# Masked attention over kept tokens on one core: seven half-size products for the outputs of batches 0 to 5, and another order of the work around the last batch

## The chip, the core and the metric

The kernel runs on one core of one Trainium2 chip. A core has engines with queues of their own: TensorE (PE in the profile; PEld is its loading of weights), VectorE (DVE), ScalarE (ACT), GpSimd (POOL) and SyncE (SP), which here only issues DMAs. Each engine takes its instructions in program order, and semaphores between them carry the dependences. TensorE's results go to PSUM, eight banks of 128 partitions by 512 floats; ScalarE and VectorE read them from there. All data are 32-bit floats. The metric is the device time of one execution in microseconds, as the median of several runs.

## The reference

The input x has 8 batches of 512 features by 1024 tokens, with a mask of zeros and ones over the tokens, about half of them one. Queries, keys and values are one and the same projection, for 8 heads of 64 features:

```python
xt = jnp.transpose(x, (0, 2, 1))
q = xt @ Wq.T
qh = q.reshape(B, T, NH, dk).transpose(0, 2, 1, 3)
scores = scale * jnp.einsum('bhqd,bhkd->bhqk', qh, qh)
cmask = mask[:, None, None, :]
rmask = mask[:, None, :, None]
logits = (scores * cmask + (1.0 - cmask) * NEG) * rmask
attn = jax.nn.softmax(logits, axis=-1)
ctx = jnp.einsum('bhqk,bhkd->bhqd', attn, qh)
ctx = ctx.transpose(0, 2, 1, 3).reshape(B, T, D)
out = ctx @ Wo.T          # returned transposed, and added to x
```

A token whose mask is one attends to the tokens whose mask is one. For a token whose mask is zero all logits are zero, so its row is the mean over all tokens, the same for all of them.

## The kernel before

**Kept tokens.** Only the kept tokens of a batch and one more, the mean, are computed: `NK` = 544 places (`SHORT`). A second build of the same function for 576 places (`LONG`) and a kernel for all tokens stand behind checks on the device and are not executed with these data. The last 32 of the 544 places are `END`; `sizes` is 128, 128, 128, 128, 32, and index `LAST` = 4 means the 32.

**The way of a batch.** x is turned (VectorE), stored to DRAM (`xd`), and the kept rows are gathered back (`gather`, GpSimd's queue). `collect` turns them on TensorE into `xc`, features by tokens. The work then goes by pairs of heads, four pairs a batch, 32 in all, numbered (batch, pair) from (0, 0) to (7, 3). Per pair: `project` (128 features of q, in two halves of 272 tokens), `turn_values`, `lengths_of` and `bias_of` (an upper bound on the scores for the exponential), `scores` with the exponentials on ScalarE (tile `e`, sums beside it), `begin_attend`, `go_on_attend` and `end_attend` (weights times values, to `cT`, 128 features by 544 tokens). `inverses` and `invert` take the inverse sums by way of DRAM to a tile `rb`, and `contexts` multiplies `cT` by it on VectorE. The last two pairs use `spread` instead, which brings the inverses to all partitions with small matmuls.

**Outputs.** `output(b, i)` takes 128 tokens (or the last 32): for each of the four `cT` of the batch a matmul of tokens by 512 output columns, accumulated in one PSUM bank, a ScalarE copy to a tile `oc`, and a store to `od` in DRAM by GpSimd's queue. The 32 tokens use four column tiles of the array, 128 output columns each. Every matmul of 32-bit floats appears as two MATMUL instructions in the profile. Later `load_rows` (SyncE) fetches x in tokens by features into tiles `g`, `fetch` (GpSimd, adding while it gathers) adds the rows of `od`, `finish_blocks` turns the sums on VectorE, and SyncE stores 2 MB to the output. For a batch b this happens in batch b + 2 (`FETCH`, `FINISH`, `ROWS`), for batch 6 in batch 7 (`FETCH_LAST`, `FINISH_LAST`, `ROWS_LAST`). The outputs of batch 7 are begun in the last pair over three of the four `cT` (`begin_output`, tile `pa`) and finished with the fourth (`end_output`); then eight gathers (`fetch_last`), TensorE transposes, the sum with x and eight stores (`finish_tokens`) end the kernel.

**The order.** It is written out by hand. A pair has five slots, k = 0 to 4; slot k begins with the scores of one block of 128 keys (the narrow block `LAST` first, then 0 to 3). `slots_of(p)` lists what else stands in each slot, and the loop in `late` puts around it, in this order: `add_ends` (k = 1), `contexts` and `invert` (k = 0), fetches, gathers, in slot 3 of pairs 1 and 3 four sums over x on ScalarE (`add_features`, line 493), then the slot's list, then loads, searches, `load_rows` and `finish_blocks`. Before each fetch and gather `keep_step` copies one element of `e` on GpSimd, so that the transfer does not start before that slot. The outputs of batch b - 1 stand in batch b: 0, 1 and the narrow one in pair 1, output 2 in pair 2, output 3 in pair 3, always slot 3.

**PSUM.** Scores use four banks (tag `s`). Tags `t` and `a` have two banks each; `bank(name)` takes one of `t` in turn, `a` serves mainly the attention's sums. In the first and the last pairs `t` and `a` are used alternately. A tile in SBUF with `bufs=n` is likewise one of n buffers in turn: `xt` (2), `oc` (5), `xin` (5), `g` (8).

## Time and profile before

| | us |
|---|---|
| median of 3 runs | 651.81 |
| lowest, highest | 649.6, 653.38 |
| the profiled execution | 656.09 |
| its span, first to last instruction | 654.4 |
| TensorE busy in it | 614.3 |
| ScalarE, VectorE, GpSimd busy | 378.3, 359.8, 211.1 |

A row of the timeline gives the start in us from the span's start, the time it took, the engine, the line of the kernel, the operation, what it writes and reads, the shape and the count; in brackets at its end stands how long the engine was idle before it and what ended that wait. Neighbouring rows of one kind are merged, and the time of a merged TensorE row reaches to the modelled end of its last matmul, so the next start is the better measure. A row of a group (no start in front) ends with busy time and mean duration in ns, then the idle time before such instructions. A row of stretches gives the busy time of each engine (count of instructions in brackets) between two times, then the granted clock of TensorE as a share, the share of DMA time and GB/s.

### The profile page before, as it was taken

The page shows a single profiled execution, that of the slowest core. Times are in us where ns is not written, and L with a number is a line of the kernel's source. Part 1 is how long each engine was busy: PE and PEld are TensorE (multiplying, and loading weights), DVE is VectorE, ACT ScalarE, POOL GpSimd, SP SyncE. Part 2 cuts the span into 40 slices and gives each one's busy share as a digit, 9 for nine tenths or more (in the row PEclk, how much of TensorE's full clock was granted, in tenths as well). Part 3 has the DMA queues.
Part 4 walks back from the last instruction along what each step waited for, and adds up shares of the span by engine and source line. Part 5 has one row for each costly group of instructions (what it writes and reads, how often), then busy time and mean ns, then how long its engine had stood idle before and what let it go on. Part 6 is the DMA issues. An engine that isn't in the chain of part 4 may idle for free. (4 is left out here: it accounts for less than half of the span.)

```text
span 654.4 us, 15913 instructions
## 1 busy us (share of the span) xinstructions
PE 614.3 (94%) x6078; PEld 380.5 (58%) x6078; DVE 359.8 (55%) x1034; ACT 378.3 (58%) x1004; POOL 211.1 (32%) x313
## 2 busy tenths in 40 slices
PE   4789799999999999999999999999999999998964
PEld 3756466656665666566665666566665666554323
DVE  6449556335465566746465558566575425444543
ACT  4266558754766577754776577664775556554400
POOL 5620400140067004830176004720275006305422
PEclk7799899999999999999999999999999999999985
DMA  7666612454588757977598756975795635566677
GB/s 237 187 199 166 233 57 67 141 168 133 147 178 214 244 172 186 180 246 230 172 182 257 228 173 155 199 244 187 196 179 164 198 102 94 111 162 188 112 220 219
DMA packets 94543, 116.62 MB, mean 178 GB/s; under 512 B 11911, under 2 KB 61639, under 8 KB 94462
## 3 DMA queue, kind: packets, MB, share of 16 engines
q1 hardware_dynamic: 74030, 75.20, 38.6%
q0 software_dynamic: 16208, 38.25, 25.2%
q10 hardware_dynamic: 4224, 2.10, 1.1%
q8 instruction: 49, 0.80, 0.5%
q14 instruction: 32, 0.26, 0.1%
HBM read 72.81 MB, written 42.70 MB: 177 GB/s over the span
## 5 line engine op out<-in xcount | busy, mean ns | idle before, releaser
L692 ACT ACTIVATE e<-s,bias 128x544 f32<-128x544 f32 x256 | 180.5, 710 | 75.6 <-PE s L684 58.9
L684 PE MATMUL s<-qT 64*64 64x272 f32 x2048 | 154.8, 398 | 6.5 <-ACT e L692 4.9
L748 PE MATMUL av<-e,v 64*64 64x272 f32 x1920 | 132.4, 392 | 0.0
L598 PE MATMUL pq<-xc,wqT 128*128 128x272 f32 x512 | 131.4, 401 | 0.0
L598 PEld LDWEIGHTS pq<-xc,wqT 128*128 128x128 f32 x512 | 93.3, 190 | 36.8 <-issue 21.0
L684 PEld LDWEIGHTS s<-qT 64*64 64x64 f32 x2048 | 77.2, 133 | 55.8 <-ACT e L692 13.4
L883 PE MATMUL po<-woT,cT 128*128 128x512 f32 (+1 forms) x448 | 108.9, 439 | 0.0
L894 POOL DMA_DIRECT2D od<-oc x56 | 30.2, 544 | 238.5 <-ACT oc L892 237.7
L977 POOL DMA_INDIRECT g<-od,block_origin x56 | 90.1, 1610 | 30.9 <-DVE ends L721 8.1
L748 PEld LDWEIGHTS av<-e,v 64*64 64x64 f32 x1920 | 76.6, 134 | 38.1 <-issue 2.1
L664 DVE TENSOR_REDUCE m<-pq 128x1 f32<-128x128 f32 x28 | 8.2, 292 | 132.0 <-ACT qT L610 107.5
L883 PEld LDWEIGHTS po<-woT,cT 128*128 128x128 f32 (+1 forms) x448 | 46.5, 149 | 54.6 <-issue 53.2
L608 ACT COPY qT<-pq 128x272 f32<-128x272 f32 x64 | 24.6, 385 | 69.7 <-PE pq L655 29.0
L947 DVE STREAM_TRANSPOSE xr<-g 128x512 f32<-128x512 f32 x56 | 57.9, 1099 | 7.6 <-DMA g<-od,block_origin 7.5
L645 DVE TENSOR_REDUCE len<-sq 128x10 f32<-128x640 f32 x32 | 25.8, 805 | 60.4 <-ACT sq L643 60.3
L974 POOL COPY step<-e 1x1 f32<-1x1 f32 x75 | 23.7, 316 | 90.7 <-ACT e L692 90.5
L692 ACT ACTIVATION_READ_ACCUMULATOR e<-s,bias 128x1 f32 x256 | 50.5, 197 | 0.0
L544 POOL DMA_INDIRECT xin<-xd,source x40 | 38.7, 968 | 16.6 <-issue 5.6
L892 ACT COPY oc<-po 128x512 f32<-128x512 f32 (+1 forms) x35 | 18.0, 515 | 44.0 <-PE po L883 43.5
L474 DVE STREAM_TRANSPOSE xt<-x 128x1024 f32<-128x1024 f32 x28 | 34.7, 1241 | 1.5 <-DMA xd<-xt 0.9
L532 DVE TENSOR_SCALAR_CACHE_REDUCE junk<-rank,key 128x1024 f32<-128x1024 f32 (+4 forms) x35 | 34.9, 998 | 0.0
L721 DVE CUSTOM_DVE_ANT_0 junk<-el,part 128x272 f32<-128x272 f32 x64 | 27.3, 427 | 6.6 <-ACT el L709 4.4
(175 smaller groups left out, 674.0 us busy)
## 6 DMA issues: line engine op xcount, KB each, us to landing
xd<-xt SPq DMA_DIRECT2D x120, 128.0 KB
x<-in_x_dram SPq DMA_DIRECT2D x56, 256.0 KB
g<-xd SPq DMA_DIRECT2D x56, 256.0 KB
out_dram<-xr SPq DMA_DIRECT2D x28, 512.0 KB
rb<-row SPq DMA_DIRECT2D x60, 160.0 KB
od<-oc POOLq DMA_DIRECT2D x28, 256.0 KB
rank<-ranks SPq DMA_DIRECT2D x6, 512.0 KB
x<-in_x_dram POOLq DMA_DIRECT2D x8, 256.0 KB
```

The source lines that it names most:

```text
L474: nc.vector.transpose(xt.rearrange("p k (d f) -> p k d f", d=ND), xs[b][r][:, :, at : at + n].rearrange("p d (k t) -> p k d t", t=Q),)
L532: nc.vector.tensor_scalar(junk[:, :n], rank[:, i * P :], key[:, col], 0.0, ALU.is_le, ALU.add, accum_out=found[:, col])
L544: nc.gpsimd.indirect_dma_start(out=xin[:n, :], out_offset=None, in_=xds[b], in_offset=bass.IndirectOffsetOnAxis(ap=searches[b][2][:n, i : ...
L598: nc.tensor.matmul(pq[:, :KH], wqT[:, d, pr * P : (pr + 1) * P], xcs[b][:, d, cols], start=(d == 0), stop=(d == ND - 1),)
L684: nc.tensor.matmul(ss[h][r * DK : (r + 1) * DK, hf, :KH], qT[heads[h], c * P + r * DK : c * P + (r + 1) * DK], qT[heads[h], queries[hf]], ...
L692: nc.scalar.activation(e[:, :, h, :], ss[h][:, :, :KH], AF.Exp, bias=bias, scale=SCALE, accum_out=sums[pair[1] % 2][:, h, c : c + 1],)
L721: nc.vector.tensor_tensor_reduce(junk[:, :KH], e[:, 0, h, :], parts[b], 1.0, 0.0, ALU.mult, ALU.add, ends[pr % 2][:, h : h + 1])
L748: nc.tensor.matmul(avs[pair][hf][head, :KH], v[keys, c, head], e[keys, hf, h, :], start=(c == 0 and not crossed), stop=(c == LAST - 1 and ...
L883: nc.tensor.matmul(po[k * n : (k + 1) * n, :w], cTs[b, pr][:, i * P : i * P + n], woT[:, pr, k * w : (k + 1) * w], start=(pr == 0), stop=( ...
L894: nc.gpsimd.dma_start(ods[b][places[i], k * w : (k + 1) * w], oc[k * n : (k + 1) * n, :w])
L947: nc.vector.transpose(xr.rearrange("p (d a) (t i) -> p a d t i", a=A, i=NT)[..., i], gs[b, i].rearrange("p (a d f) -> p a d f", a=A, f=Q),)
L977: nc.gpsimd.indirect_dma_start(out=gs[b, i], out_offset=None, in_=ods[b], in_offset=bass.IndirectOffsetOnAxis(ap=block_origin[:, b, i : i ...
```

## The change

For the build with 544 places, the outputs of batches 0 to 5 (made in batches 1 to 6) are computed for the 512 full places as one product of two 512 by 512 matrices by seven products of quarter matrices (256 tokens x 256 features x 256 columns) and sums before and after. `combine_weights` forms four sums of quarters of the output weights on GpSimd, once, in pair (1, 0). `combine_tokens` forms four sums of quarters of the tokens on VectorE, in slots 1 and 2 of pair 1, into two `xt` tiles. `product(b, i)` computes one product in one bank, as eight MATMUL instructions, and adds it into four tiles c11, c12, c21, c22 (tag `oc`): product 1 is copied by ScalarE, all other sums are VectorE's, reading PSUM; each finished quarter is stored by GpSimd's queue, 256 rows of 256 columns. Products 1, 6, 7, 5 stand in slot 3 of pair 1, then the narrow output, then the projection, which there takes a bank of `a`; products 2 and 3 in pair 2; product 4 in pair 3.

Around the last batch: all outputs of batch 6 are made in pair (7, 1): output 0 in slot 2, outputs 1 and 2 in slot 3, output 3 and the narrow one in slot 4, where before output 2 stood in slot 4 of (7, 1), output 3 in slot 1 and the narrow one in slot 3 of (7, 2). Loads, fetches and transposes of batch 6 move earlier with it. In the last pair the spread and the contexts of the pair before stand in slot 0, not 1, and the five partial products in slots 1, 2, 3, 4, 4, not 1, 1, 2, 3, 4. The partial and the final product of the last 32 tokens use four column tiles of 128 columns, with the columns read in another order, and their store becomes four DMAs on SyncE's and ScalarE's queues in turn.

```diff
@@ -319,6 +319,7 @@
     G = NB // P
     A = P // Q
     NQ = 4
+    in_halves = n == SHORT
     NC = -(-LONG // P)
     LAST = NC - 1
     LP = LAST * P
@@ -893,44 +894,156 @@
         for k in range(parts):
             nc.gpsimd.dma_start(ods[b][places[i], k * w : (k + 1) * w], oc[k * n : (k + 1) * n, :w])
 
+    HALF = D // 2
+    both = {}
+    if n == SHORT:
+        for i in range(1, 5):
+            both["t", i] = keep.tile([P, 2, HALF], F32, name=f"t_{i}")
+
+    def combine_weights():
+
+        left = [woT[:, 0:2, 0:HALF], woT[:, 2:4, 0:HALF]]
+        right = [woT[:, 0:2, HALF:D], woT[:, 2:4, HALF:D]]
+        t1, t2, t3, t4 = (both["t", i] for i in range(1, 5))
+        nc.gpsimd.tensor_tensor(t1, right[0], left[0], ALU.subtract)
+        nc.gpsimd.tensor_tensor(t2, right[1], t1, ALU.subtract)
+        nc.gpsimd.tensor_tensor(t3, right[1], right[0], ALU.subtract)
+        nc.gpsimd.tensor_tensor(t4, t2, left[1], ALU.subtract)
+
+    def combine_tokens(b, i):
+
+        if i in (1, 3):
+            t = sb.tile([P, T // NQ // Q, P], F32, tag="xt", name=f"st_{b}_{i}", bufs=2)
+            t = t.rearrange("p k c -> p (k c)").rearrange("p (s j n) -> p s j n", s=2, j=2)
+            both["s", i], both["s", i + 1] = t[:, 0], t[:, 1]
+        for j in range(2):
+            early, late_ = cTs[b, j], cTs[b, 2 + j]
+            to = both["s", i][:, j, :]
+            upper, lower = slice(0, 2 * P), slice(2 * P, 4 * P)
+            if i == 1:
+                nc.vector.tensor_tensor(to, early[:, lower], late_[:, lower], ALU.add)
+            elif i == 2:
+                nc.vector.tensor_tensor(to, both["s", 1][:, j, :], early[:, upper], ALU.subtract)
+            elif i == 3:
+                nc.vector.tensor_tensor(to, early[:, upper], early[:, lower], ALU.subtract)
+            else:
+                nc.vector.tensor_tensor(to, late_[:, upper], both["s", 2][:, j, :], ALU.subtract)
+
+    def product(b, i):
+
+        def tokens(j, m):
+            cols = slice(m * P, (m + 1) * P)
+            if i in (3, 5, 6, 7):
+                return both["s", {3: 4, 5: 1, 6: 2, 7: 3}[i]][:, j, cols]
+            first = 2 * P if i == 4 else 0
+            cols = slice(first + m * P, first + (m + 1) * P)
+            return cTs[b, j if i == 1 else 2 + j][:, cols]
+
+        def features(j):
+            if i == 1:
+                return woT[:, j, 0:HALF]
+            if i == 2:
+                return woT[:, 2 + j, 0:HALF]
+            if i == 3:
+                return woT[:, 2 + j, HALF:D]
+            return both["t", {4: 4, 5: 1, 6: 2, 7: 3}[i]][:, j, :]
+
+        po = bank(f"po_{b}_{i}")
+        for m in range(2):
+            for j in range(2):
+                nc.tensor.matmul(
+                    po[:, m * HALF : (m + 1) * HALF],
+                    tokens(j, m),
+                    features(j),
+                    start=(j == 0),
+                    stop=(j == 1),
+                )
+
+        def new(name):
+            t = both[name] = sb.tile([P, D], F32, tag="oc", name=f"{name}_{b}", bufs=NC)
+            return t
+
+        def store(t, row, col):
+            rows = slice(END + row * 2 * P, END + (row + 1) * 2 * P)
+            nc.gpsimd.dma_start(
+                ods[b][rows, col * HALF : (col + 1) * HALF].rearrange("(m p) c -> p m c", p=P),
+                t.rearrange("p (m c) -> p m c", m=2),
+            )
+
+        add = nc.vector.tensor_tensor
+        if i == 1:
+            ods[b] = dr.tile([NK, D], F32, tag="od", name=f"od_{b}")
+            nc.scalar.copy(new("c11"), po)
+        elif i == 6:
+            add(new("c12"), po, both["c11"], ALU.add)
+        elif i == 7:
+            add(new("c21"), po, both["c12"], ALU.add)
+        elif i == 5:
+            add(new("c22"), po, both["c21"], ALU.add)
+            add(both["c12"], po, both["c12"], ALU.add)
+            store(both["c22"], 1, 1)
+        elif i == 2:
+            add(both["c11"], po, both["c11"], ALU.add)
+            store(both["c11"], 0, 0)
+        elif i == 3:
+            add(both["c12"], po, both["c12"], ALU.add)
+            store(both["c12"], 0, 1)
+        else:
+            add(both["c21"], both["c21"], po, ALU.subtract)
+            store(both["c21"], 1, 0)
+
     partials = {}
 
+    def add_product(b, i, pr, po, start, stop):
+
+        n = sizes[i]
+        parts = P // n
+        w = D // parts
+        tokens = cTs[b, pr][:, i * P : i * P + n]
+        if parts == 1:
+            nc.tensor.matmul(po, tokens, woT[:, pr, :], start=start, stop=stop)
+            return
+        in_order = woT[:, pr, :].rearrange("p (a d f) -> p d a f", a=A, d=ND)
+        for k in range(parts):
+            nc.tensor.matmul(
+                po[k * n : (k + 1) * n, :w],
+                tokens,
+                in_order[:, k * ND // parts : (k + 1) * ND // parts, :, :],
+                start=start,
+                stop=stop,
+            )
+
     def begin_output(b, i):
 
-        n = sizes[i]
         po = bank(f"pa_{b}_{i}")
         for pr in range(ND - 1):
-            nc.tensor.matmul(
-                po[:n, :],
-                cTs[b, pr][:, i * P : i * P + n],
-                woT[:, pr, :],
-                start=(pr == 0),
-                stop=(pr == ND - 2),
-            )
+            add_product(b, i, pr, po, pr == 0, pr == ND - 2)
+        w = D // (P // sizes[i])
         pa = sb.tile([P, D], F32, tag="xin", name=f"pa_{b}_{i}", bufs=NC)
-        nc.scalar.copy(pa[:n, :], po[:n, :])
+        nc.scalar.copy(pa[:, :w], po[:, :w])
         partials[i] = pa
 
     def end_output(b, i):
         n = sizes[i]
+        parts = P // n
+        w = D // parts
         if i == 0:
             ods[b] = dr.tile([NK, D], F32, tag="od", name=f"od_{b}")
         po = bank(f"po_{b}_{i}")
-        nc.tensor.matmul(
-            po[:n, :],
-            cTs[b, ND - 1][:, i * P : i * P + n],
-            woT[:, ND - 1, :],
-            start=True,
-            stop=True,
-        )
+        add_product(b, i, ND - 1, po, True, True)
         oc = sb.tile([P, D], F32, tag="oc", name=f"oc_{b}_{i}", bufs=NC)
-        nc.vector.tensor_tensor(
-            oc[:n, :].rearrange("p (d a f) -> p a d f", d=ND, a=A),
-            po[:n, :].rearrange("p (a d f) -> p a d f", d=ND, a=A),
-            partials[i][:n, :].rearrange("p (a d f) -> p a d f", d=ND, a=A),
-            ALU.add,
-        )
-        nc.sync.dma_start(ods[b][places[i], :], oc[:n, :])
+        if parts == 1:
+            nc.vector.tensor_tensor(
+                oc.rearrange("p (d a f) -> p a d f", d=ND, a=A),
+                po.rearrange("p (a d f) -> p a d f", d=ND, a=A),
+                partials[i].rearrange("p (a d f) -> p a d f", d=ND, a=A),
+                ALU.add,
+            )
+        else:
+            nc.vector.tensor_tensor(oc[:, :w], po[:, :w], partials[i][:, :w], ALU.add)
+        for k in range(parts):
+            queue = nc.scalar if k % 2 else nc.sync
+            queue.dma_start(ods[b][places[i], k * w : (k + 1) * w], oc[k * n : (k + 1) * n, :w])
 
     def in_blocks(t):
         return t.rearrange("(k f) (a n) -> a f k n", f=Q, a=A)
@@ -1035,12 +1148,25 @@
             do(0, go_on_attend, before)
         due = []
         if pr == 1 and b + 1 == B:
-            due = [0, 1]
-        elif pr > 0 and 0 < b < B - 1:
+            due = [1, 2]
+            do(2, output, b - 1, 0)
+        elif pr > 0 and 0 < b < B - 1 and not in_halves:
             due = {1: (0, 1, LAST), 2: (2,), 3: (3,)}[pr]
+        halves = ()
+        if in_halves and 0 < b < B - 1:
+            halves = ((), (1, 6, 7, 5), (2, 3), (4,))[pr]
+            if pr == 1:
+                for k, i in ((1, 1), (1, 2), (2, 3), (2, 4)):
+                    do(k, combine_tokens, b - 1, i)
         if not new:
+            for i in halves:
+                do(3, product, b - 1, i)
+            if halves and pr == 1:
+                do(3, output, b - 1, LAST)
             for i in due:
                 do(3, output, b - 1, i)
+        if in_halves and p == ND:
+            do(0, combine_weights)
         if p == 0:
             do(0, project, behind, 1)
             do(1, values, behind)
@@ -1070,6 +1196,8 @@
             do(3, collect, b + 1, 3, None, "a")
             do(3, collect, b + 1, 4, by_vector)
             do(3, lengths_of, behind)
+            for i in halves:
+                do(3, product, b - 1, i)
             for i in due:
                 do(3, output, b - 1, i)
             do(3, project_with_top, 0)
@@ -1078,22 +1206,21 @@
             do(1, project_with_values)
             do(2, lengths_of, behind)
             do(2, end_attend, before)
-            do(3, project_with_top, 1)
+            do(3, project_with_top, 1, "a" if halves and pr == 1 else "t")
         elif behind:
-            do(1, output, b - 1, LAST - 1)
             do(1, values, behind)
             do(2, lengths_of, behind)
             do(2, end_attend, before)
             do(3, bias_of, behind)
-            do(3, output, b - 1, LAST)
         if p == ND - 1:
             for d in range(ND):
                 do(3 + d // 2, turn_weights, woT, "wo", d, None, "at"[d // 2], True)
         if pr == 1 and b + 1 == B:
-            do(4, output, b - 1, 2)
+            do(4, output, b - 1, LAST - 1)
+            do(4, output, b - 1, LAST)
         if p + 1 == len(pairs):
             for i in range(NC):
-                do((1, 1, 2, 3, 4)[i], begin_output, b, i)
+                do((1, 2, 3, 4, 4)[i], begin_output, b, i)
         return todo
 
     def load_weights(w, nm, queue=None):
@@ -1300,10 +1427,10 @@
             (1, 1): (6, 7),
         }
         FINISH = {(0, 4): (0, 1), (1, 1): (2, 3), (1, 2): (4, 5), (1, 4): (6, 7)}
-        FETCH_LAST = {(2, 4): (0, 1, 2), (3, 0): (3, 4, 5), (3, 1): (6, 7)}
-        FINISH_LAST = {(3, 1): (0, 1, 2), (3, 2): (3, 4, 5), (3, 3): (6, 7)}
+        FETCH_LAST = {(2, 0): (0,), (2, 1): (1, 2), (2, 2): (3, 4), (2, 3): (5, 6), (2, 4): (7,)}
+        FINISH_LAST = {(2, 3): (0,), (2, 4): (1, 2), (3, 1): (3, 4, 5), (3, 2): (6, 7)}
         ROWS = {(2, 2): (0, 1), (2, 3): (2, 3), (3, 0): (4, 5), (3, 2): (6, 7)}
-        ROWS_LAST = {(2, 0): (0, 1, 2), (2, 1): (3, 4, 5), (2, 2): (6, 7)}
+        ROWS_LAST = {(1, 2): (0, 1), (1, 3): (2, 3), (1, 4): (4, 5), (2, 0): (6, 7)}
         for p, pair in enumerate(pairs):
             b, pr = pair
             before = pairs[p - 1] if p else None
@@ -1319,10 +1446,9 @@
                         invert(before)
                     else:
                         inv = inverses(before)
-                if p + 1 == len(pairs):
-                    if k == 1:
-                        spread(before, inv)
-                        contexts(before)
+                if p + 1 == len(pairs) and k == 0:
+                    spread(before, inv)
+                    contexts(before)
                 if b > 1:
                     for i in FETCH.get((pr, k), ()):
                         keep_step(pair, c)
```

4 lines of the change are left out of this document (2 added, 2 removed).

## The prediction

> **What bounds the kernel now.** I read the page first, then the busy time by stretch, then the timelines of TensorE, ScalarE and VectorE for one batch and for the end. The stretches below are one batch (from its first output product to the next batch's), the last pair, and the tail.
>
> ```profile
> span 654.4 us, 15913 instructions
> PE 614.3 (94%) x6078; PEld 380.5 (58%) x6078; DVE 359.8 (55%) x1034; ACT 378.3 (58%) x1004; POOL 211.1 (32%) x313
> ...
> core 0: us, PE busy (x) PEld busy (x) DVE busy (x) ACT busy (x) POOL busy (x), PEclk, DMA share, GB/s
> 200.36:272.67 72.31, 72.06 (x755) 44.72 (x751) 44.62 (x127) 46.79 (x127) 25.81 (x37) 1.00 0.74 203
> ...
> 597.50:631.20 33.70, 30.75 (x180) 12.90 (x180) 18.25 (x37) 10.41 (x26) 13.31 (x15) 1.00 0.71 135
> 631.20:654.40 23.20, 8.96 (x33) 5.80 (x33) 6.49 (x15) 0.00 (x0) 7.64 (x8) 0.54 0.72 219
> ```
>
> A middle batch (here batch 2's products to batch 3's) takes 72.31 us and TensorE is busy for 72.06 of them, at a granted clock of 1.00. So matmul time saved there is time saved, and a wait added to TensorE is time lost, one for one. Only the last pair (33.70 us, 30.75 busy) and the tail have slack. The profiled execution took 656.09 us for its span of 654.4; the median of the runs is 651.81, 0.7% below, and I carry differences over to it.
>
> **Products: what they save.** TensorE in batch 6 (pairs 1 and 3) and in batch 7:
>
> ```profile
> 489.44 8.14 PE L883 MATMUL po<-woT,cT 128*128 128x512 f32 x48
> 497.51 2.10 PE L598 MATMUL pq<-xc,wqT 128*128 128x272 f32 x8
> ...
> 531.27 3.70 PE L883 MATMUL po<-woT,cT 128*128 128x512 f32 x8
> 534.81 2.00 PE L598 MATMUL pq<-xc,wqT 128*128 128x272 f32 x8
> 536.64 0.27 PE L655 MATMUL pq<-ident,top 128*128 128x128 f32 x1
> ...
> 561.69 7.13 PE L883 MATMUL po<-woT,cT 128*128 128x512 f32 x16
> 568.66 2.00 PE L598 MATMUL pq<-xc,wqT 128*128 128x272 f32 x8
> 588.59 1.08 PE L883 MATMUL po<-woT,cT 128*32 128x128 f32 x32
> 589.60 1.15 PE L684 MATMUL s<-qT 64*64 64x272 f32 x16
> ```
>
> From start to next start, sixteen instructions of 512 columns take 6.97 us, eight take 3.54, so one takes 0.43 and about 0.1 goes to the change of tile shape; eight of 272 columns take 1.83 (229 ns each). For 256 columns I take 214 ns, half of 427 and just below the line through the two; the upper bound is 229, if weight loads set the pace. A product is 2 token blocks x 2 feature chunks x 2 instructions = 8, so 1.71 us. Seven make 12.0 against 13.65 for the four outputs (32 x 427): 1.7 us saved per batch, 10.2 over six. By place: pair 1 gives up two outputs for four products (0), pair 2 one for two (0), pair 3 one for one (-1.71). At 229 ns the saving is 0.85 per batch, 5 in all.
>
> The Trainium skill ("TensorE: Matmul & The Clock Gate", section Back-to-back issue gap) gives a warm gap of N/2.4 + 2.5 ns. If each instruction is two passes, an estimate from that page is 432 and 218 ns, which would save 1.6 us per batch instead of 1.7 and make the sum below 0.6 us later; the trace's 229 ns for 272 columns agrees with the page's 232.
>
> **Products: what they wait for.** They use two banks in turn ("t"); a bank is free once its product is evacuated. A bank used to be wanted every 3.5 us, now every 1.71. ScalarE, then VectorE, during slots 1 to 3 of pair 1 of batch 6; the last VectorE row is the second pair of transposes in batch 2:
>
> ```profile
> 491.00 0.62 ACT L493 ACTIVATE junka<-x 128x512 f32<-128x512 f32 x1
> ...
> 493.79 0.18 ACT L493 ACTIVATION_READ_ACCUMULATOR junka<-x 128x1 f32 x1
> 493.88 0.56 ACT L892 COPY oc<-po 128x512 f32<-128x512 f32 x1
> ```
>
> ```profile
> 487.99 2.05 DVE L947 STREAM_TRANSPOSE xr<-g 128x512 f32<-128x512 f32 x2
> ...
> 490.75 2.04 DVE L947 STREAM_TRANSPOSE xr<-g 128x512 f32<-128x512 f32 x2
> 500.32 0.29 DVE L664 TENSOR_REDUCE m<-pq 128x1 f32<-128x128 f32 x1 [7.53 <-ACT qT L610]
> ...
> 202.65 2.04 DVE L947 STREAM_TRANSPOSE xr<-g 128x512 f32<-128x512 f32 x2
> ```
>
> The four L493 sums stand ahead of the output copies in slot 3. Product 1 ends 1.8 us after 489.44, but its copy to c11 cannot start before 493.88 and ends at +5.0. Products 1 and 6 have filled both banks by +3.5, so product 7 starts at +5.05: a wait of 1.5 us in each of six batches.
>
> Then VectorE, on which eight new sums of 128x256 stand in slots 1 and 2. The nearest prices:
>
> ```profile
> 623.43 0.38 DVE L800 TENSOR_TENSOR cT<-av,rb 128x272 f32<-128x272 f32 x1
> 625.75 0.44 DVE L800 TENSOR_TENSOR cT<-av,rb 128x272 f32<-128x272 f32 x1 [1.95 <-PE av L730]
> L927 DVE TENSOR_TENSOR oc<-po,pa 128x512 f32<-128x512 f32 x4 | 2.8, 691 | 1.1 <-PE po L919 1.1
> L401 POOL TENSOR_SCALAR part<-count,kept 64x272 f32<-64x272 f32 x16 | 15.5, 970 | 5.3 <-DMA xin<-xd,source 4.7
> ```
>
> At 0.40 us (between the two L800 rows; 0.32 if they overlap, 0.46 if each waits for the one before) they add 3.2 us. The transposes of slot 2, which stand before product 6's sum, end at 492.79 - 489.44 = +3.35 now and at +6.5 then; in batch 2, whose products start at 200.36, they end at +4.33 now and +7.5 then. The sum needs 0.7 (L927) and frees the bank of product 5. So product 5 starts at about +8.2 in batch 2, +7.9 in 4 (nearly as late), +7.3 in 6, and at +6.8, right behind product 7, where the transposes come earlier (3, 5) or are absent (1). From there 1.71 for it and 0.93 for the narrow output: the projection starts at +9.4 to +10.9 instead of +8.07 (497.51). The losses of batches 1 to 6 are 1.3, 2.8, 1.4, 2.5, 1.3 and 1.9, 11.2 us against the 10.2 saved. **Products: +1 us.** The bounds are -5 (VectorE hides everything and the bank wait is halved) and +9 (229 ns, 0.46 us).
>
> Elsewhere the swaps cost nothing I can find: in pair 2 the sums follow each product by 0.7 us, before the second bank after it is wanted, and in pair 3 the L493 sums end before the shorter slot's scores need ScalarE. ScalarE loses three copies per batch. GpSimd's four weight sums (from below 1 us to above 4 each, by L401 for half the size) come once, two pairs before they are used, with only later gathers queued behind. On GpSimd's DMA queue the stores stay as many; the first of pair 1 now waits for product 5's sum, behind it only the narrow stores and the query masks of the next batch; that pair's gathers are issued by then.
>
> **The last batch.** TensorE, then VectorE, GpSimd and SyncE there, and ScalarE's exponential:
>
> ```profile
> 588.34 0.32 PE L655 MATMUL top<-ident,top 128*128 128x128 f32 x1 [0.54 <-DVE top L652]
> 597.49 1.13 PE L684 MATMUL s<-qT 64*64 64x272 f32 x12 [0.81 <-ACT el L709]
> 602.74 3.70 PE L903 MATMUL pa<-woT,cT 128*128 128x512 f32 x8 [0.95 <-DVE cT L867]
> 615.14 2.76 PE L903 MATMUL pa<-woT,cT 128*32 128x512 f32 x6
> 620.28 1.31 PE L810 MATMUL rb<-ident,ris 128*64 128x128 f32 x20 [1.31 <-DVE ris L831]
> 625.64 4.87 PE L919 MATMUL po<-woT,cT 128*128 128x512 f32 x10
> ```
>
> ```profile
> 603.37 1.11 DVE L947 STREAM_TRANSPOSE xr<-g 128x512 f32<-128x512 f32 x1 [0.50 <-DMA g<-od,block_origin]
> ...
> 618.19 1.10 DVE L947 STREAM_TRANSPOSE xr<-g 128x512 f32<-128x512 f32 x1 [0.16 <-DMA g<-od,block_origin]
> ...
> 590.29 1.99 POOL L894 DMA_DIRECT2D od<-oc  x4 [5.90 <-ACT oc L892]
> 598.27 1.70 POOL L977 DMA_INDIRECT g<-od,block_origin  x1 [5.82 <-DVE ends L721]
> 632.96 1.00 POOL L963 DMA_INDIRECT g<-od,origin  x1 [19.56 <-DMA od<-oc]
> ...
> 619.32 5.28 SPq L954 DMA_DIRECT2D out_dram<-xr  x4
> ...
> L692 ACT ACTIVATE e<-s,bias 128x544 f32<-128x544 f32 x256 | 180.5, 710 | 75.6 <-PE s L684 58.9
> L692 ACT ACTIVATION_READ_ACCUMULATOR e<-s,bias 128x1 f32 x256 | 50.5, 197 | 0.0
> ```
>
> - The partial product of the last 32 tokens goes to four column tiles: 24 instructions at the rate of 588.59 (1.01 us for 32) take 0.75 us, not 2.7: **-2.0**. Its final product, a fifth of 4.87, shrinks alike: **-0.6**.
> - The wait of 1.31 goes: VectorE inverts late because batch 6's transposes (to 619.29) stand ahead; they come earlier now, and the partial products cover the last exponentials: **-1.3**.
> - With the spread one slot earlier most of the wait of 0.95 goes: **-0.6**.
> - Batch 6's last outputs (3.5 and 1.0 us) leave pair 2, where they covered waits: a score block follows the exponentials of the one before (2 x 0.91 us), and the top's transpose follows ScalarE's squares. I count waits of 0.8, 0.9 and 1.0, less the 0.54 and 0.81 that are there now: **+1.3**.
> - The fetches start in pair 2, and three transposes now stand on VectorE ahead of the contexts and inverses that the spread needs. The narrow output would end near 580 (568.66, plus output 3.5, projection 2, scores 1, output 3.5, itself 1.0). Its store and what follows took 8 us to the first fetch (590.29 to 598.27), and that fetch 5.1 to land (603.37). With two more fetches at 2 us each the third transpose can start at 594 to 598; contexts and inverses take some 3 us more, and TensorE wants them near 598: a wait of 0 to 4, I take **+1.7**.
> - The 2 MB store at 619.32 is gone when the last outputs are stored, so they land sooner before the gather of 632.96: **-0.5** (0 to -1.5). The narrow store's four pieces go over SyncE's and ScalarE's queues, with only the three other stores behind them. All after 632.96 (21.4 us) keeps its length.
>
> **Last batch: -2 us** (-5 to +1). The sum: +1 - 2 = -1 us.
>
> **The rivals.**
> 1. *VectorE late: slower.* Each microsecond more on VectorE ahead of product 6's sum goes into TensorE in batches 2 to 6. At 0.7 us a sum (L927's price for twice the length) it is 2.4 us more each, 5 x 2.4 = 12: 663. It decides from 0.9 us up (5 x 0.9, less the 1). Against it stand the L800 rows.
> 2. *VectorE not in the way: faster.* If the sums slip into its gaps, only ScalarE's wait stays, 6 x (1.35 - 1.7) = -2, and with fetches in time the last batch gives -4: 646. For it: VectorE waits 7.5 us before 500.32.
> 3. *The rearranged batch gives nothing*, because the fetches come late: last batch +1, products +1: 654, still no change.
> 4. *The clock.* Waits of 1.5 to 3 us per batch might lower the granted clock; half of it for 3 us in six batches is +9: 660. Against it: the stretch with the 1.31 wait held 1.00; for it: the tail, with 8.96 of 23.20 us busy, had 0.54. The Trainium skill ("TensorE: Matmul & The Clock Gate", section Why this matters for your kernels) warns of idle gaps over about 3 us; the trace agrees so far as it goes, and by that rule these waits stay just under it.
>
> **How the numbers follow.** The runs shown go from 649.6 to 653.38, so 0.5% (3.3 us) is about what can be told from no change. Forecast, 0.38, and rival 3, 0.06: same 0.44. Rival 2: faster 0.31. Rival 1, 0.21, and rival 4, 0.04: slower 0.25. The time is 651.81 - 1 = 650.8. The range reaches past rival 2 (646) and half way to rival 1 (663).
>
> **What would show it.** Right: product 7 waits some 1.5 us for the c11 copy on ScalarE and product 5 for VectorE in batches 2, 4 and 6; a middle batch stays near 72 us; the last spread no longer waits for the inverses. Wrong: 256-column instructions at 229 ns or more, no waits at the products, or a wait of several microseconds at the first spread of the last pair.

## The result, and the profile after

The changed kernel takes 661.2 us (median of 4 runs, 658.56 to 664.5) where the kernel before, beside it, takes 650.7: the medians lie 10.5 us apart, and the ratio over all runs is put at 1.0145 (95% interval 1.011 to 1.018), so it is slower, clear of noise. The prediction, 650.8 with a range of 645 to 657.5, was wrong. The profiled execution of the changed kernel took 661.41 us for a span of 659.7. (The profiled execution before was 5 us above its median, and the excess lies ahead of the first output products, which start at 128.2 us there and at 122.39 after, so stretches are compared below, not spans.)

Stretches of the changed kernel: from batch 2's products to batch 3's, then to batch 4's (columns as in the row of stretches before).

```profile
core 0: us, PE busy (x) PEld busy (x) DVE busy (x) ACT busy (x) POOL busy (x), PEclk, DMA share, GB/s
194.44:267.47 73.03, 70.97 (x778) 49.33 (x774) 48.59 (x134) 45.07 (x124) 26.86 (x36) 1.00 0.75 200
267.47:343.72 76.25, 72.89 (x779) 50.33 (x775) 51.62 (x149) 45.07 (x124) 27.88 (x37) 0.98 0.72 193
```

TensorE has less to do (70.97 us busy where it had 72.06), and the batch is longer: it waits now. The six batches of the products, from one first product to the next (the last one to the scores of slot 2 in pair (7, 1)), took 72.2 to 72.3 us each, the last stretch 68.4; now they differ from that by -0.1, +0.7, +4.0, +0.8, +0.7 and +0.7, together +6.8. From the scores of slot 2 in pair (7, 1) to the end it was 96.5 us (557.87 to 654.4) and is 100.8 (558.88 to 659.7): +4.3. These two sums, 11.1 us together in the two profiled executions, are the whole loss.

The waits of TensorE in the changed kernel, by what ended them (total us, times, longest):

```profile
PE rb L811 <- DVE ris L832: 7.5, 1, 7.5
...
PE po L954 <- ACT c L976: 5.4, 4, 1.3
PE po L954 <- DVE c L978: 4.2, 5, 2.1
```

None of them is in the list of before, where the longest wait at an output or a spread is 1.3 us. In pair 1 of batch 6, on TensorE:

```profile
489.73 1.99 PE L954 MATMUL po<-woT,cT 128*128 128x256 f32 x8
491.56 1.89 PE L954 MATMUL po<-t,st 128*128 128x256 f32 x8
494.79 1.99 PE L954 MATMUL po<-t,st 128*128 128x256 f32 x8 [1.34 <-ACT c L976]
497.28 1.99 PE L954 MATMUL po<-t,st 128*128 128x256 f32 x8 [0.49 <-DVE c L978]
499.20 1.08 PE L884 MATMUL po<-woT,cT 128*32 128x128 f32 x32
```

These are products 1, 6, 7, 5 and the narrow output. Product 7 waits for the copy of product 1 (ScalarE, L976), product 5 for product 6's sum (VectorE, L978). A wait costs more than its bracket says, because the bracket counts from the modelled end of the product ahead (1.89 us after its start), and a product that waits for nothing starts 1.73 us after the one ahead: product 7 starts 3.23 us after product 6, which is 1.50 lost for a wait of 1.34, and product 5 comes 0.76 later for a wait of 0.49. The list has the wait for the copy four times, in batches 2, 4, 5 and 6; in batch 1 the same wait, 1.33 us, is put down to GpSimd, and in batch 3 VectorE's sums of the tokens end last. Batch 3, the worst one, on TensorE and on VectorE:

```profile
269.73 1.99 PE L954 MATMUL po<-t,st 128*128 128x256 f32 x8 [0.26 <-DVE st L926]
272.54 1.99 PE L954 MATMUL po<-t,st 128*128 128x256 f32 x8 [0.82 <-DVE st L928]
276.63 3.64 PE L954 MATMUL po<-t,st 128*128 128x256 f32 x8 [2.10 <-DVE c L978]
```

```profile
264.02 0.23 DVE L860 TENSOR_TENSOR rb<-rb 128x64 f32<-128x64 f32 x1 [4.54 <-DMA rb<-row]
...
268.58 0.75 DVE L924 TENSOR_TENSOR st<-cT,cT 128x256 f32<-128x256 f32 x2
...
274.05 2.01 DVE L1060 STREAM_TRANSPOSE xr<-g 128x512 f32<-128x512 f32 x2
275.91 0.67 DVE L978 TENSOR_TENSOR c<-po,c 128x512 f32<-128x512 f32 x1
```

There VectorE waits 4.54 us for the tile `rb` from DRAM before it can begin contexts, sums and transposes; products 6, 7 and 5 all wait, and after the wait of 2.10 us product 5 takes 3.64 us, not 1.99, at a granted clock of 0.50 (276.63 to 278.50). Around the last pair's first spread, TensorE, the stretch of the spread (granted clock 0.50), VectorE, then GpSimd:

```profile
606.22 2.40 PE L811 MATMUL rb<-ident,ris 128*64 128x128 f32 x20 [7.53 <-DVE ris L832]
608.55 2.09 PE L685 MATMUL s<-qT 64*64 64x272 f32 x16
...
626.90 1.26 PE L811 MATMUL rb<-ident,ris 128*64 128x128 f32 x20
```

```profile
606.22:608.55 2.33, 2.33 (x21) 2.00 (x21) 0.04 (x1) 0.31 (x1) 0.00 (x0) 0.50 0.64 110
```

```profile
595.60 1.12 DVE L1060 STREAM_TRANSPOSE xr<-g 128x512 f32<-128x512 f32 x1 [3.67 <-DMA g<-od,block_origin]
599.30 1.09 DVE L1060 STREAM_TRANSPOSE xr<-g 128x512 f32<-128x512 f32 x1 [2.58 <-DMA g<-od,block_origin]
601.86 1.09 DVE L1060 STREAM_TRANSPOSE xr<-g 128x512 f32<-128x512 f32 x1 [1.47 <-DMA g<-od,block_origin]
602.81 0.20 DVE L860 TENSOR_TENSOR rb<-rb 128x64 f32<-128x64 f32 x1
...
606.08 0.18 DVE L833 TENSOR_SCALAR ris<-ends,pads 128x2 f32<-128x2 f32 x1
```

```profile
581.92 2.00 POOL L895 DMA_DIRECT2D od<-oc  x4 [0.17 <-issue]
590.12 1.69 POOL L1090 DMA_INDIRECT g<-od,block_origin  x1 [5.99 <-ACT sq L644]
```

Read from the bottom: the narrow store is issued at 581.92, the first fetch 8.2 us later, and it has landed at 595.60; the next two land 3.7 and 2.6 us apart. Only behind the third transpose come the contexts and inverses (602.81 to 606.26), and TensorE, ready at 598.7, waits 7.53 us. Spread and scores then take 2.33 and 2.02 us from start to start, where 1.24 and 1.08 are usual: 2.0 us more at a granted clock of 0.50. The wait at the second spread (1.31 before) is gone.

### The profile page after: what moved, and what is told of

The parts are those of the page before. It is cut to its first block, busy times and chain, and to the rows that moved or that the text cites. A ratio compares the mean times of both kernels' runs of the same rounds, so it can differ in the third digit from the quotient of the medians.

```text
span 659.7 us, 16321 instructions
## 1 busy us (share of the span) xinstructions
PE 610.7 (93%) x6246; PEld 411.4 (62%) x6246; DVE 402.0 (61%) x1124; ACT 367.9 (56%) x986; POOL 225.4 (34%) x317
## 5 line engine op out<-in xcount | busy, mean ns | idle before, releaser
L1090 POOL DMA_INDIRECT g<-od,block_origin x56 | 91.7, 1637 | 31.4 <-issue 12.5
L968 POOL DMA_DIRECT2D od<-c x24 | 18.2, 757 | 211.5 <-DVE c L992 81.8
L954 PE MATMUL po<-t,st 128*128 128x256 f32 x144 | 36.7, 401 | 11.9 <-ACT c L976 5.4
L1087 POOL COPY step<-e 1x1 f32<-1x1 f32 x77 | 27.5, 357 | 52.1 <-ACT e L693 51.5
L954 PEld LDWEIGHTS po<-t,st 128*128 128x128 f32 x144 | 27.4, 197 | 20.2 <-ACT c L976 8.2
L494 ACT ACTIVATE junka<-x 128x512 f32<-128x512 f32 x48 | 30.2, 629 | 1.1
L893 ACT COPY oc<-po 128x128 f32<-128x128 f32 (+1 forms) x11 | 4.2, 383 | 45.9 <-PE po L884 45.9
```

The lines of the kernel that those rows point to most:

```text
L494: nc.scalar.activation(junk, xs[b][r][:, d, :], AF.Copy, accum_out=xbars[b][:, d, r : r + 1])
L954: nc.tensor.matmul(po[:, m * HALF : (m + 1) * HALF], tokens(j, m), features(j), start=(j == 0), stop=(j == 1),)
L1087: nc.gpsimd.tensor_copy(step, es[pair, c][0:1, 0, 0, 0:1])
L1090: nc.gpsimd.indirect_dma_start(out=gs[b, i], out_offset=None, in_=ods[b], in_offset=bass.IndirectOffsetOnAxis(ap=block_origin[:, b, i : i ...
```

## The experiments

Each ratio is to the kernel before on the same chip, with its 95% interval. The line numbers are those of the kernel run.

**The two parts alone.** One kernel has the changed products and the last batch as before; the other the rearranged last batch and the outputs of before, by one switch (shown alone):

```diff
-    in_halves = n == SHORT
+    in_halves = False
```

> The seven products for batches 0 to 5 as in the change, everything around the last batch as before. Theory (the two parts add up; the traces put +0.7 us on each of batches 2, 4, 5 and 6, +4 on batch 3, and +4.3 on the stretch from pair (7, 1) to the end): 3 to 7 us slower than before, 654 to 658. Rival (the loss lies in the last batch alone and batch 3 was an accident): within 1 us of before plus the four times 0.7, at most 654. In the trace: the wait of 1.34 us for the c11 copy in each batch in either case; no wait near 7.5 us at the first spread of the last pair.

> The outputs of batches 0 to 5 as before (four products of 512 columns), the last batch rearranged as in the change. Theory: the wait of 7.5 us at the first spread of the last pair stays and the end gains 3 us, so +3 to +5 us, 654 to 656. Rival (the wait comes only from being late after the products): no wait there, 2 to 4 us faster than before, 647 to 649.

Measured: products alone 655.69 us, 1.0064 (1.0039 to 1.0090); last batch alone 655.49, 1.0067 (1.0040 to 1.0094). By itself the one loses 4.8 us and the other 4.6, together 9.4 of the 10.5. Of the products alone, product 5 in batch 2, the batch that lost most there (74.11 us, where batch 3 took 72.99); of the last batch alone, the first spread:

```profile
204.89 1.99 PE L954 MATMUL po<-t,st 128*128 128x256 f32 x8 [1.62 <-DVE c L978]
```

```profile
603.73 2.40 PE L811 MATMUL rb<-ident,ris 128*64 128x128 f32 x20 [7.55 <-DVE ris L832]
```

**Cost of a column.** In the kernel before, output 1 is cut into two pieces of 256 columns, output 2 into four of 128, output 3 into 320 and 192. The reason tested is a floor by the loading of weights, which would make the 256-column instruction dearer than half of the 512-column one (shortened):

```diff
+        cuts = [[512], [256, 256], [128] * 4, [320, 192]][i]
+        for cut in cuts:
+            for pr in range(ND):
+                nc.tensor.matmul(po[:, at : at + cut], cTs[b, pr][:, tokens_of_i], woT[:, pr, at : at + cut], ...)
+            at += cut
```

> The kernel before with the outputs of batches 0 to 5 cut by columns and nothing else: output 0 whole (512), output 1 in two matmuls of 256, output 2 in four of 128, output 3 in 320 and 192, all by the same weights as before, loaded again for each. It measures the disputed price of an instruction by itself, without sums or waits. Theory (the loading of weights sets a floor per instruction near 229 ns): sixteen instructions of 256 columns take 3.65 us, thirty-two of 128 take 7.3. Rival (time goes with the columns, as the prediction's sum had it, and the 229 ns in the changed kernel come from its operands): 3.4 us and 3.4 to 3.7. 320 + 192: 3.5 to 4.0 under the theory.

```profile
486.90 3.70 PE L896 MATMUL po<-woT,cT 128*128 128x512 f32 x8
490.44 3.62 PE L886 MATMUL po<-woT,cT 128*128 128x256 f32 x16
493.99 1.08 PE L896 MATMUL po<-woT,cT 128*32 128x128 f32 x32
...
509.94 3.84 PE L886 MATMUL po<-woT,cT 128*128 128x128 f32 x32
513.61 2.00 PE L598 MATMUL pq<-xc,wqT 128*128 128x272 f32 x8
...
528.90 3.72 PE L886 MATMUL po<-woT,cT 128*128 128x320 f32 x16
532.46 2.00 PE L598 MATMUL pq<-xc,wqT 128*128 128x272 f32 x8
```

The kernel took 654.67 us in its one run, within the 648.88 to 656.06 of the kernel before, so only its rows are read. Start to start: 3.54, 3.55, 3.67 and 3.56 us for the same work in 8, 16, 32 and 16 instructions. Time goes with the columns down to 128 (115 ns); there is no floor at 256. So the products do save what was forecast, and the theory of dearer instructions falls.

**The waits at the products.** Three kernels have the products and the last batch of before. One puts the four sums over x on ScalarE behind product 1, so that the copy to c11 goes first; one moves `finish_blocks` 4 and 5 from slot 2 to slot 3, behind the sums of the products on VectorE; one does both (shortened: the loop that held the sums over x leaves them out there):

```diff
             for i in halves:
                 do(3, product, b - 1, i)
+                if i == 1:
+                    for j in range(G):
+                        do(3, add_features, b + 1, G + j)
-        FINISH = {(0, 4): (0, 1), (1, 1): (2, 3), (1, 2): (4, 5), (1, 4): (6, 7)}
+        FINISH = {(0, 4): (0, 1), (1, 1): (2, 3), (1, 3): (4, 5), (1, 4): (6, 7)}
```

> Products alone, with ScalarE's four sums over x in slot 3 of pair 1 moved behind the c11 copy, so that product 7's bank comes free about 2.6 us earlier. Theory (two waits in a row: without ScalarE's, product 5 waits longer for VectorE, whose queue ends where it did): product 7 waits for nothing, product 5 for 1.8 us or more, in batches 2 to 6 the time of a batch falls by at most 0.3 us; only batch 1 gains its 1.3. Total 1 to 3 us below products alone, 653 to 654.5. Rival (ScalarE's wait is the loss): 6 x 1.34 = 8 us below, 647 to 648.

> Products alone, with the two transposes of slot 2 of pair 1 moved behind the products of slot 3, so that VectorE reaches product 6's sum 2 us earlier. Theory: product 5's wait (0.5 to 1.6 us) goes, ScalarE's wait of 1.34 stays: 2.5 to 5 us below products alone, 651 to 653. Rival (the moved transposes hold back the maximum for the bias or the next contexts): as much lost again in slot 4, no change.

> Both moves at once. Theory (the products are worth 56 x 229 ns against 32 x 440 once nothing waits): no wait at the products, a batch takes 71.1 us instead of 72.3, six batches 6 to 8 us below before, 643 to 645. Rival (evacuating a bank every 1.83 us is too much for two banks whatever the queues): waits of over 0.5 us per batch remain and the time stays above 648.

Measured: 657.45 us, 1.0081 (1.0052 to 1.0111), with the sums later; 649.85, 0.9992 (0.9965 to 1.0018), with the transposes later; 645.51, 0.9916 (0.9883 to 0.9949), with both. In this order, batches 2 and 3 of the first, batch 2 of the second, and batch 1 of the third, where products 6, 7 and 5 follow without a wait:

```profile
204.81 3.68 PE L954 MATMUL po<-t,st 128*128 128x256 f32 x8 [2.31 <-DVE c L978]
...
280.78 1.99 PE L954 MATMUL po<-t,st 128*128 128x256 f32 x8 [2.31 <-DVE c L978]
```

```profile
199.41 3.72 PE L954 MATMUL po<-t,st 128*128 128x256 f32 x16 [1.34 <-ACT c L976]
```

```profile
124.88 5.34 PE L954 MATMUL po<-t,st 128*128 128x256 f32 x24
```

The two waits stand in series before the same deadline. Without ScalarE's, TensorE arrives sooner and waits 2.31 us for VectorE instead: nothing gained, rather lost where the clock halves (3.68 against 1.99 us behind equal waits); the 653 to 654.5 us expected were not reached. Without VectorE's, only ScalarE's 1.34 remains and a batch takes 72.1 to 72.2 us, about what it took before; that alone is 0.7% below the products as they were. Without both, the batches take 70.5 to 71.8 us; waits of up to 0.50 us for VectorE are left in three of them. The kernel of both moves, measured again beside a later run:

> The products with both moves and the last batch as before, the kernel of the run with ratio 0.9916, now on the same chip as the run beside it. Theory: its gain lies in batches 1 to 6, where no transfer is waited for, so it does not depend on the chip: ratio 0.988 to 0.995 again. Rival: the gain goes on a chip with slower transfers, as it did for the same products with the rearranged last batch: ratio 0.998 or more.

It took 646.5 us, 0.9911 (0.9877 to 0.9944): the gain holds on another chip.

**The first spread.** Batch 6's transposes go from before the contexts to slots 1 and 2 of the last pair, once with all of the change, once with the last batch alone.

```diff
-        FINISH_LAST = {(2, 3): (0,), (2, 4): (1, 2), (3, 1): (3, 4, 5), (3, 2): (6, 7)}
+        FINISH_LAST = {(3, 1): (0, 1, 2, 3), (3, 2): (4, 5, 6, 7)}
```

> The change with one edit: the three transposes of batch 6 that stood in slots 3 and 4 of pair (7, 2) move to slots 1 and 2 of pair (7, 3), behind the contexts and inverses on VectorE. Theory (VectorE stands waiting for the fetches and holds back the inverses): the 7.5 us wait goes down to below 1, 6 to 7 us faster than the change, 654 to 655. Rival (the inverses wait for the row that SyncE brings by way of DRAM, or for something else): the wait stays above 4 us and the time within 2 us of the change's.

> The outputs of batches 0 to 5 as before, the last batch rearranged, the three transposes later as in the run beside this one. Theory: 2 to 4 us faster than before, 647 to 649, since the narrow partial product (2 us), the wait of 1.31 us and the narrow final product (0.6) are gone and nothing is lost. Rival (uncovering pair (7, 2) costs what the rest gains): within 1 us of before.

Measured: 654.9 us, 1.0072 (1.0041 to 1.0102), and 649.79, 0.9971 (0.9948 to 0.9995). The medians are 6.3 and 5.7 us below the same kernel without the move, but the wait is halved, not gone. The first spread in both, and VectorE ahead of it in the second:

```profile
600.72 2.40 PE L811 MATMUL rb<-ident,ris 128*64 128x128 f32 x20 [3.74 <-DVE ris L832]
```

```profile
596.82 1.31 PE L811 MATMUL rb<-ident,ris 128*64 128x128 f32 x20 [3.07 <-DVE ris L832]
598.06 2.01 PE L685 MATMUL s<-qT 64*64 64x272 f32 x16
```

```profile
593.36 0.23 DVE L860 TENSOR_TENSOR rb<-rb 128x64 f32<-128x64 f32 x1 [6.22 <-DMA rb<-row]
...
596.56 0.20 DVE L832 RECIPROCAL ris<-sums 128x8 f32<-128x8 f32 x1
```

Behind the transposes a second thing was late: the inverses of pair (7, 1), which go by way of DRAM to `rb`. SyncE issues them behind batch 5's last 2 MB of stores. Is it these stores? One kernel lets them wait until the inverses are out (with the last batch alone, and with everything), beside everything without it:

```diff
-                while rests:
+                while rests and not (b + 1 == B and (pr, k) == (1, 4)):
```

> The last batch rearranged alone, with batch 6's transposes in the last pair's slots 1 and 2 (as in the run that took 649.8), and now the four stores of batch 5's last 2 MB are issued one slot later, behind SyncE's loads and stores of the inverses of pair (7, 1), not ahead of them. Theory: the 3.07 us that TensorE still waits at the first spread are the row of inverses, held back by those 2 MB; the rb tile lands up to 3 us earlier than 593.36, the wait drops below 1 us, and the time by 2 to 3, to 647. Rival: the row is late for a reason of its own (the round trip through DRAM), the wait stays near 3 us and the time at 650, and the stores are then in the way of the fetches.

> The whole change with all three moves: sums over x behind product 1, batch b - 2's second transposes one slot later, batch 6's transposes in the last pair's slots 1 and 2. Theory: the two parts are independent, so the gains add: 645.5 with the products in that form is 5.2 below the kernel before, 649.8 with the last batch in that form is 0.9 below it, together 644.6 (643 to 646.5). Rival: they share something at the end (VectorE, the DMA queues), and it gives no more than the products alone, 645.5 or more, with a wait over 3.1 us at the first spread.

> The same with batch 5's stores behind the inverses of pair (7, 1) as well. Theory: if the 2 MB hold back the row of inverses, 2 to 3 us less than the same kernel without that move, about 642. Rival: no difference between the two.

Measured, on a chip where the kernel before took 654.59: 653.41 us, 0.9968 (0.9943 to 0.9994); 655.85, 1.0008 (0.9979 to 1.0036); 652.47, 0.9946 (0.9914 to 0.9979). The third is 3.4 us below the second, near the 2 to 3 expected, but neither comes to the 642 or 644.6 us. The first kernel, TensorE and VectorE (its profiled execution, 658.89 us, is the longest of its twelve):

```profile
598.63 1.31 PE L811 MATMUL rb<-ident,ris 128*64 128x128 f32 x20
...
623.15 2.40 PE L811 MATMUL rb<-ident,ris 128*64 128x128 f32 x20 [5.94 <-DVE ris L833]
```

```profile
614.50 7.56 DVE L1060 STREAM_TRANSPOSE xr<-g 128x512 f32<-128x512 f32 x8 [10.86 <-DMA out_dram<-xr]
```

The first spread no longer waits: from the first store of the inverses to the issue of their return it is 4.6 us there (582.10 to 586.67), and 7.9 in the changed kernel (584.40 to 592.31). So the stores were what held the inverses. But the stores, now among the fetches, read the one buffer of `xr` until 614.50; batch 6's transposes wait for it 10.86 us and the second spread 5.94: given back. And the second kernel shows that the gains did not add there: `rb` landed later still.

```profile
599.87 0.23 DVE L860 TENSOR_TENSOR rb<-rb 128x64 f32<-128x64 f32 x1 [10.35 <-DMA rb<-row]
```

So the inverses were given to GpSimd's queue, for pair (7, 1) alone, which has room until the first fetch:

```diff
+        queue = nc.gpsimd if pair == (B - 1, 1) else nc.sync
-            nc.sync.dma_start(
+            queue.dma_start(
```

> The whole change with the three moves, and the inverses of pair (7, 1) stored and loaded by GpSimd's queue, not behind batch 5's last 2 MB on SyncE's. Theory: without that the rb tile was issued at 593.25 and landed at 599.87, behind 2 MB, and TensorE waited 7.11 us at the first spread; on GpSimd's queue only the 32 narrow rows stand ahead of it, it lands before 592, the wait at the first spread goes below 1 us, batch 5's stores still end early enough that the transposes need not wait for the tile xr, and the second spread has no wait over 1 us. 6 to 9 us less than the same kernel without it (ratio 1.0008), so a ratio of 0.987 to 0.992. Rival: the round trip through DRAM is slow whatever the queue, because the DMA engines are full: rb lands near 599 again, a wait of 5 us or more stays and the ratio is near 1.00.

Measured: 645.07 us, 0.992 (0.9883 to 0.9957). The time came out at the edge of what the theory gave, the wait did not: below 1 us was expected. The first spread, and GpSimd:

```profile
589.00 2.40 PE L811 MATMUL rb<-ident,ris 128*64 128x128 f32 x20 [4.06 <-DVE ris L832]
```

```profile
570.74 1.56 POOL L846 DMA_DIRECT2D row<-rt  x3 [0.58 <-DVE rt L842]
575.92 0.52 POOL L846 DMA_DIRECT2D row<-rt  x1 [3.63 <-DMA od<-oc]
581.93 1.08 POOL L851 DMA_DIRECT2D rb<-row  x2 [5.48 <-DMA row<-rt]
```

The round trip took no less on this queue: 11.2 us from the first store to the issue of the return, of which one of the four stores was held back for 3.63 us by earlier output stores of this queue. So the rival had a part; whether the 2 MB on the other queue slow it too is not shown apart from these stores. Counted from the scores of slot 2 in (7, 1), `rb` came 3 us earlier than in the kernel of 1.0008 (40.4 against 43.5 us), and the wait is 3 us shorter; the expectation had set its time, before 592, on the other execution's clock, in which all of this lies later. The two ratios are from two chips. The products with both moves and the last batch as before had 0.9911 beside it, so the rearranged batch gave nothing yet. What the spread needs is VectorE's own sums, which are there before TensorE wants them (582.37 against 585.59 in the first kernel below); it stands behind the contexts of (7, 1) only by the order of VectorE's work. Both last kernels put these contexts behind the first spread, with the inverses on SyncE's queue and on GpSimd's:

```diff
-                if k == 0 and p > 1:
+                if k == 0 and 1 < p < len(pairs) - 1:
                     contexts(pairs[p - 2])
...
                     spread(before, inv)
+                    contexts(pairs[p - 2])
                     contexts(before)
```

> The whole change with the three moves (the kernel of ratio 1.0008), the inverses on SyncE's queue as in the change, but in the last pair the contexts of pair (7, 1), which need the late rb tile, stand on VectorE behind the inverses of (7, 2) and the first spread, not ahead of them. Theory: the spread needs nothing but VectorE's own sums and was held back only because VectorE takes its work in order; the first spread starts without a wait (below 0.5 us), the score block behind it too, and what is left of rb's lateness is a wait at the first partial product, 4 us less than the 4 to 7 us before (the spread's 1.3 and the scores' 1.5 fit in, and the contexts of both pairs follow each other): ratio 0.988 to 0.995. Rival: rb is so late that the same time is lost at the partial product: ratio 0.998 or more.

> The same with the inverses of pair (7, 1) on GpSimd's queue (the kernel of ratio 0.992, which still waited 4.06 us at the first spread). Theory: no wait at the first spread, at most 2 us at the first partial product, so 2 to 4 us less than with the contexts ahead: ratio 0.986 to 0.990. Rival: the contexts in front were not what held the spread, and the ratio stays at 0.992 with the wait moved to the partial product.

Measured: 642.11 us, 0.987 (0.9835 to 0.9905), and 645.09, 0.9916 (0.9886 to 0.9945). The first, TensorE and VectorE:

```profile
585.59 1.31 PE L811 MATMUL rb<-ident,ris 128*64 128x128 f32 x20
...
590.24 1.13 PE L1004 MATMUL pa<-woT,cT 128*128 128x512 f32 x2 [1.20 <-DVE cT L868]
592.40 1.55 PE L1004 MATMUL pa<-woT,cT 128*128 128x512 f32 x2 [1.03 <-DVE cT L868]
```

```profile
582.19 0.18 DVE L833 TENSOR_SCALAR ris<-ends,pads 128x2 f32<-128x2 f32 x1
588.13 0.23 DVE L860 TENSOR_TENSOR rb<-rb 128x64 f32<-128x64 f32 x1 [5.77 <-DMA rb<-row]
```

The inverses are ready at 582.37, the spread starts at 585.59 without a wait, and of the lateness of `rb` 1.20 and 1.03 us are left at the first partial product. Counted from the scores of slot 2 in (7, 1) again, `rb` comes after 42.3 us here and came after 43.5 in the kernel of 1.0008, so it is nearly as late; but the spread starts after 39.7 us and not 46.9, and the first final product after 67.8 and not 72.0. On one and the same chip, with the inverses on GpSimd's queue, the first final product comes after 65.2 us and not 69.7. So the order of VectorE's work is worth some 4 us up to there; the rest of the step from 1.0008 to 0.987 lies outside this stretch, and the two were run on different chips. To the end it is 94.8 us (545.86 to 640.7), 1.7 below the kernel before. This kernel has the lowest ratio of the study, 1.3% below the kernel before: the change as it stood, with four pieces of work in another place. Its interval overlaps that of the products with both moves and the last batch as before, on the same chip (0.9877 to 0.9944), so the products' part of the gain is shown, and the last batch's is not settled. The other one missed what was expected (0.986 to 0.990): its partial product waits only 0.19 us, but its second spread waits 1.03, and from its first final product to the end it takes 30.1 us (608.94 to 639.0), not 27.0 (613.66 to 640.7). Why its end is longer was not followed, and this profiled execution, 640.77 us, is the fastest of its six, so it doesn't show why the median is 645.09; the two intervals overlap as well.

## Why the prediction was wrong

**What the products save** (10.2 us): right. The start-to-start time of a product is 1.73 us (515.15 to 516.98 to 518.71 in pair 2 of batch 6 gave 1.83, with the change of tile shape, and 1.73); 1.71 was forecast, and batch 1 without its waits (in the kernel of both moves) took 70.49 us, 1.69 below its 72.18. The 229 ns bound is refuted by the cut outputs.

**Product 7 behind ScalarE** (1.5 us in each batch): right in place and size, 3.23 - 1.73 = 1.50 in batch 6, but for batch 3, where VectorE came last. In batch 1 too it was ScalarE: with the sums over x behind the copy that batch took 70.50 us, not 72.05.

**Product 5 behind VectorE**: right as a mechanism, too small in its terms. With 1.7 saved per batch, the losses of batches 1 to 6 were 1.6, 2.4, 5.7, 2.5, 2.4 and 2.4, together 17.0, where 1.3, 2.8, 1.4, 2.5, 1.3 and 1.9, together 11.2, were forecast; 4.3 of the 5.8 too little lie in batch 3. The price of a sum was not the reason: a pair of them takes 0.75 us, some 0.33 each, below the 0.40 taken. What failed is the statement that in batches 3 and 5 the transposes come earlier and product 5 starts right behind product 7. VectorE's work before product 6's sum begins when `rb` has landed, and that differs from run to run: here batch 3 waited 4.54 us for it and lost most, in the products alone batch 2, with 4.24 us. In batch 3 half the clock, 1.7 us, came on top of it. Why `rb` landed late there was not followed. "Products +1" was +6.8.

**The last batch** (-2 us): the mechanism was named, and its term is the one that failed most. For the first spread 0 to 4 us were given, 1.7 taken; measured were 7.53 and 2.0 more at half the clock. Piece by piece: the first fetch was put at 588 (580 and 8 us) and came at 590.12; it was to land 5.1 us later, and did after 5.5; the next two were to follow 2 us apart, and were 3.1 apart on average; contexts and inverses took 3.45 us where 3 were taken; TensorE was ready at 598.7, as forecast (598). So the spacing of the fetches and the start added up, each a little late. The forecast's own pieces (588, 5.1, twice 2, the third transpose's 1.1 and 3) already make 601.2, a wait of 3.2 us; 1.7 was taken, for which it gives no reason. And the forecast saw one cover only: the run without the transposes in front showed the inverses of (7, 1), held back by 2 MB on the same queue, late behind them, and a wait of 3.07 to 3.74 us left.

The other terms of the last batch came out better than forecast: -5.2 us (4.3 less 9.5) against -3.7. Pair (7, 2), for which +1.3 was set, took about +0.2: from the scores of slot 2 in (7, 1) to the first spread, without its wait, 39.8 us now, and 40.7 before with a score block of 1.08 more in it. The partial product of the 32 tokens and both waits at the spreads went about as forecast (-4.2 against -3.9), the end from the first final product on shrank by 1.3 (28.8 to 27.5 us, against 1.1).

**The rivals.** "VectorE late" (663 us) has the right place, but at a third of a microsecond per sum, not 0.7. "The clock" is true in part: after waits of 2.1 to 7.5 us some matmuls ran at half the clock, which cost 1.7 us in batch 3 and 2.0 in the last pair, not in every batch; that its 660 us comes near the 661.2 measured is luck. The Trainium skill ("TensorE: Matmul & The Clock Gate", section Why this matters for your kernels) warns of gaps over about 3 us; the trace agrees for the wait of 3.07 us (the scores right behind that spread took 1.94 us from start to start, not 1.08), but half the clock stands after a wait of 2.10 as well, and there the measurement decides. "The rearranged batch gives nothing" named the cause, the late fetches, at +1 us where the last batch came to +4.3. "VectorE not in the way" was not tried as it was meant, with ScalarE's wait left and -4 us from the last batch: the nearest run, the transposes later, gave 0.8 us for the products' part where 2 were forecast. That the two moves took 645.5, near its 646, is luck, since there ScalarE's wait is gone too and the last batch is as before. The sign was missed because gain and loss of the products were nearly equal in the sum, so that 5.8 us more of waits decided it, and because the one open wait of the last batch was taken below the middle of 0 to 4 us and came out above its end.

## What to carry to other kernels

When a step on the bounding engine gets shorter, list the engines that must empty its banks and what stands ahead of each evacuation in program order: the next deadline comes sooner, and late engines hide behind each other. Taking away the first wait alone only showed the next and gained nothing here; taking away the later one gained 0.7%, and both 1.5%. When transfers are moved earlier, put behind them on an in-order engine only work that really needs them: here moving the contexts behind the spread took some 4 us off the way to the first final product, with the transfer nearly as late as before.

## What the runs showed of the hardware

Half the clock did not follow from the length of a wait alone: of two waits of 2.31 us at the same product of one kernel, one was followed by a product of 3.68 us at a granted clock of 0.53, the other by one of 1.99 at 1.00 with all behind it at the usual pace. In the kernel with the contexts behind the spread two short waits, 1.20 and 1.03 us, with 1.1 us of matmuls between them, were enough: the scores behind took 2.03 us, not 1.08, at 0.50. What decides was not tried.

Time of a 32-bit matmul went with its columns from 512 down to 128 (443 ns at 512, 115 ns at 128, changes of shape included), though the weights were loaded four times as often.

A round trip of small transfers through DRAM, from the first store to the issue of the return, took 7.9 us behind 2 MB of stores on the same queue and 4.6 with these stores put behind it. On GpSimd's queue, where it also stood behind other stores, it took 11.2.
